# One tile for the output's sums, weight sums and additions at other slots, a branch's number loaded sooner, and two changes of order

## The chip, the cores and the metric

The kernel runs on one core of a Trainium2 chip. The metric is the device time of one execution in microseconds. Five engines work side by side and wait for each other by semaphores: TensorE (PE, with its weight loads PEld), VectorE (DVE), ScalarE (ACT), GpSimd (POOL) and SyncE (SP, which here only issues DMAs).

## The reference

A block of two layers on x of 8 x 256 tokens, 512 wide, all in float32:

```
xn = layernorm(x)
x  = x + attention0(xn) + ffn0(xn)      # layer 1
xn = layernorm(x)
x  = x + attention1(xn) + ffn1(xn)      # layer 2
```

`attention0` is a linear attention with 32 heads of 128 and decays: q, k, v = silu(xn @ W), scores weighted by a decay, the output normalized by its root mean square over all heads, multiplied by a weight and by sigmoid(xn @ Wg), and projected back to 512. `ffn0` routes each token to 2 of 16 experts, beside a shared expert. `attention1` is a softmax attention with one head of 128, `ffn1` a low-rank mixture: 16 of 64 rank-16 pairs for each token.

## The kernel before

**Opening.** The 2048 tokens are taken in four chunks of 512 (`NCH` = 4, `TPC` = 4 tiles of 128). Each chunk is normalized, turned with TensorE (`turn_rows`: four transposes into a PSUM bank, then a copy to SBUF, on VectorE for even tiles and on ScalarE, L282, for odd ones), routed, and sent through the shared expert (`shared_up`, `shared_down`). `decays` computes the decay tiles with ScalarE's Exp (L406) and stores them. Then VectorE works out which token goes to which slot of which expert. The opening's tiles lie in a pool, `opening`, that is closed behind that work; the attention's pool takes the same memory.

**Attention of layer 1.** Four passes, one for each chunk (`i`), of eight units, one for each group of four heads (`g`). A unit is seven `Outer` products (`ORDER`: p1, p2, p6, p5, p3, p7, p4; `k` counts them), and each of these again seven products of 8 matmuls of 128x128x128 (L738). This is a fast scheme of matrix multiplication with seven products in place of eight, used twice. The sums that it needs of weights and tokens are made in the first pass and stored in DRAM for the others. `copied` (L1112) takes a bank to SBUF with ScalarE; `result` adds banks and copies into the tiles a, b, c, d of the unit, on VectorE and GpSimd (all through `add`, L101). For p7, r is added to c on GpSimd and to a on VectorE; the additions to a are held in `self.added` and all made at the third quarter of the result, (1, 1), the last at (0, 1).

When a tile is whole, a `Quarter` begins: silu and gate on ScalarE (L835 to L842), `scores` (L860, L861, weighted into `s` on VectorE), `attend` (L872, L873), the squares `sq` (ScalarE, L884) that GpSimd adds into `sums`, and the gated output `gT`. `project` (L950) multiplies `gT` with the output weights `wo`, again in seven products p1 to p7, and adds each to its slice of the tile `acc`; in a pass's first unit it copies instead, on ScalarE (L958). At a pass's end `combine` (GpSimd) makes the four output blocks of the seven sums, in place, and `finish` (VectorE, L649) scales them and adds them to the tokens' sum. `acc` is made anew for each pass, in a pool with one buffer.

In the second pass (`i` = 1) `out_sum` makes the four weight sums p7, p5, p6 and p4 of each unit's `wo` on GpSimd and stores them in `wos`, from which later passes load.

**The order.** Within the attention ScalarE and GpSimd follow the program's order; TensorE, VectorE and SyncE are ordered by the framework's scheduler, which takes what is ready, in the program's order where several are. `keep_in_program_order` pins an instruction behind what was traced before it on its engine. Small steps are queued by hand: `later(n, f)` puts f into a list, and `slot()`, called after each product, runs what is due; there are 49 slots in a unit. Per slot one step runs, or two if more than 12 are waiting; names in a list (`out_sum`, `combine` and others) do not count.

**Experts.** From the second pass on, experts' tiles are gathered and computed between the products. 36 tiles are usual; a branch (`beyond`, L1215 and L1216) runs more if the data need them. Its number, `used`, is loaded into the engines' registers just ahead of the branch, in unit 3 of the last pass.

**Layer 2.** For each chunk: `low_rank` twice (L1614), then seven products (L1711) by `seven`, which runs lists of other work (`fill`) between its products: transposes of the next chunk (`turned`, L279), its routing (L1503), projections (L1492) and softmax.

## Time and profile before

| | |
|---|---|
| median of 3 runs | 2756.16 us (2751.43 to 2757.16) |
| profiled execution | 2759.92 us, span 2758.2 us |
| PE busy | 2704.0 us (98%) |
| VectorE, GpSimd, ScalarE busy | 1597.3, 1652.5, 943.9 us |
| matmuls | 19250 |
| granted clock of TensorE | 0.994 |

The profile is of one execution, which took longer than each of the three runs that were timed. Busy times are unions of the instructions' spans; an engine's idle time is told with what ended it. A line such as L101 is that of a helper (`tt`), so groups are told apart by their tiles, whose buffer numbers are left out. The opening lasts to about 120 us, the attention's four passes to about 2460 us, layer 2 to the end.

### The profile page before, as it was taken

Reading aid. Unit: us, or ns where it says so; the run is one execution under the profiler, and the core shown is the slowest. Engines: PE = TensorE matmul, PEld = TensorE weight load, DVE = VectorE, ACT = ScalarE, POOL = GpSimd, SP = SyncE. Lnnn points to the kernel's source line nnn. Section 1 sums busy time; section 2 is a strip of 40 time slices with the busy share of each in tenths; the row PEclk is TensorE's granted clock in tenths of the full one; section 3 lists DMA queues with packets and bytes.
Section 4 is the critical chain, followed back from the end, with each engine's and each line's share of the span. In section 5 each row is a group of like instructions: output and inputs, shape, how many; then the busy total and the mean of one; then the engine's idle time right before and its main releaser. Section 6 shows DMA issues by size and latency. Waiting matters only on the chain. (4 is left out here: it accounts for less than half of the span.)

```text
span 2758.2 us, 48688 instructions
## 1 busy us (share of the span) xinstructions
PE 2704.0 (98%) x19250; PEld 2499.6 (91%) x19250; DVE 1597.3 (58%) x2701; ACT 943.9 (34%) x1672; POOL 1652.5 (60%) x1509
## 2 busy tenths in 40 slices
PE   9999999999999999999999999999999999999999
PEld 5699999999999999999999999999998999987877
DVE  7656777776545555555545555555454555667663
ACT  5232222222343333333433333334433333432211
POOL 6478777776466767666755555656655567653210
PEclk9999999999999999999999999999999999999999
DMA  7898888888888777667777776787776688653211
GB/s 290 314 345 323 317 330 330 326 319 323 340 286 293 265 277 275 256 243 285 279 255 260 252 260 251 265 297 254 267 266 231 241 301 300 220 222 104 75 60 64
DMA packets 150872, 721.46 MB, mean 262 GB/s; under 512 B 18240, under 2 KB 24768, under 8 KB 108096
## 3 DMA queue, kind: packets, MB, share of 16 engines
q1 hardware_dynamic: 135824, 661.89, 65.2%
q0 software_dynamic: 14528, 55.88, 6.1%
q8 instruction: 154, 2.52, 0.4%
q14 instruction: 78, 0.64, 0.1%
q10 hardware_dynamic: 288, 0.52, 0.1%
HBM read 576.29 MB, written 144.04 MB: 261 GB/s over the span
## 5 line engine op out<-in xcount | busy, mean ns | idle before, releaser
L738 PE MATMUL ps_a<-xt,w 128*128 128x128 f32 x5376 | 752.1, 277 | 16.6 <-ACT cp L1112 11.8
L738 PEld LDWEIGHTS ps_a<-xt,w 128*128 128x128 f32 x5376 | 687.3, 193 | 44.5 <-ACT cp L1112 16.0
L101 POOL TENSOR_TENSOR c<-c,r 128x512 f32<-128x512 f32 x264 | 362.4, 1396 | 161.2 <-DVE r L101 157.7
L101 POOL TENSOR_TENSOR c<-c 128x512 f32<-128x512 f32 x240 | 305.8, 1286 | 254.4 <-DVE c L101 230.5
L1112 ACT COPY cp<-ps_a 128x512 f32<-128x512 f32 x384 | 224.2, 584 | 645.9 <-PE ps_a L738 620.0
L738 PE MATMUL ps_e<-xt,w 128*128 128x128 f32 x2688 | 376.1, 277 | 0.2 <-DVE r L101 0.2
L101 POOL TENSOR_TENSOR sums<-sums,sq 128x256 f32<-128x256 f32 x240 | 180.3, 751 | 307.7 <-ACT sq L884 297.9
L738 PE MATMUL ps_a<-w,xt 128*128 128x128 f32 x1792 | 348.0, 276 | 0.0
L738 PEld LDWEIGHTS ps_e<-xt,w 128*128 128x128 f32 x2688 | 342.9, 193 | 3.6 <-DVE r L101 0.4
L101 POOL TENSOR_TENSOR w<-w 128x512 f32<-128x512 f32 x224 | 298.2, 1339 | 76.4 <-DVE w L101 29.1
L950 PE MATMUL ps_sc<-wo,gT 128*128 128x256 f32 x1288 | 306.9, 382 | 5.2 <-PEq L1216 3.8
L738 PEld LDWEIGHTS ps_a<-w,xt 128*128 128x128 f32 x1792 | 273.3, 193 | 0.0
L101 DVE TENSOR_TENSOR acc<-ps_sc,acc 128x512 f32<-128x512 f32 x208 | 142.7, 689 | 207.0 <-PE ps_sc L950 164.2
L950 PEld LDWEIGHTS ps_sc<-wo,gT 128*128 128x128 f32 x1288 | 233.9, 192 | 31.6 <-issue 4.4
L893 DVE SCALAR_TENSOR_TENSOR gT<-ps_o,nw,c 128x256 f32<-128x256 f32 x256 | 112.0, 479 | 231.0 <-ACT sq L884 230.9
L738 PE MATMUL ps_b<-xt,w 128*128 128x128 f32 x1536 | 215.6, 277 | 6.0 <-issue 3.8
L101 DVE TENSOR_TENSOR c<-ps_a,c 128x512 f32<-128x512 f32 x216 | 146.8, 687 | 123.3 <-PE ps_a L738 117.6
L835 ACT ACTIVATE c<-c 128x512 f32<-128x512 f32 x256 | 150.2, 628 | 165.5 <-DVE c L101 108.0
L884 ACT ACTIVATE sq<-ps_o 128x512 f32<-128x512 f32 x128 | 76.5, 597 | 380.2 <-PE ps_o L873 371.8
L738 PEld LDWEIGHTS ps_b<-xt,w 128*128 128x128 f32 x1536 | 196.5, 193 | 9.2 <-issue 5.6
L101 DVE TENSOR_TENSOR s<-ps_sc,decay 128x384 f32<-128x384 f32 x256 | 139.1, 552 | 75.7 <-PE ps_sc L861 74.1
L738 PE MATMUL ps_e<-w,xt 128*128 128x128 f32 x896 | 174.1, 276 | 0.0
(296 smaller groups left out, 4581.7 us busy)
## 6 DMA issues: line engine op xcount, KB each, us to landing
w<-in_w_att_dram SPq DMA_DIRECT2D x56, 1024.0 KB
w<-in_w_att_dram SPq DMA_DIRECT2D x72, 768.0 KB
st<-in_w_att_dram SPq DMA_DIRECT2D x32, 1024.0 KB
wo<-in_w_out_dram SPq DMA_DIRECT2D x113, 256.0 KB
decay<-dec SPq DMA_DIRECT2D x64, 384.0 KB
w<-ws0p SPq DMA_DIRECT2D x12, 1792.0 KB
w<-ws1p SPq DMA_DIRECT2D x12, 1792.0 KB
w<-ws2p SPq DMA_DIRECT2D x12, 1792.0 KB
```

Source lines behind the costliest of these rows:

```text
L101: (eng or nc.vector).tensor_tensor(o, a, b, op)
L738: mm(bank[:, bass.ts(ty, P)], a, b, start=(first and ty == 0), stop=True, skip_group_check=True,)
L835: nc.scalar.activation(qk, qk, AF.Silu)
L884: nc.scalar.activation(sq, po, AF.Square)
L893: nc.vector.scalar_tensor_tensor(gT[:, h, :].rearrange("p (t n) -> p t n", t=2), po[:, bass.ts(h, S)].rearrange("p (t n) -> p t n", t=2), ...
L950: mm(py[:, bass.ts(t, S)], self.O[p][:, hh, bass.ts(t, P)], self.wo[p][:, hh, :], start=(t == 0 and hh == 0), stop=(hh == 1), skip_group_c ...
L1112: nc.scalar.copy(c, bank)
```

## The change

- `acc` becomes one tile for all passes, made once (`sums_of_seven`).
- The load of p3's output weights is asked for at `k` = 4 of a unit instead of 5; `out_sum`'s four steps are queued from there, 6, 22, 24 and 26 slots later, instead of 6, 8, 10 and 12 slots after `k` = 5.
- p7's additions to a: at (1, 1) the first is made at once and the next two one and two slots later (`add_a`, a name that does not count); the one of (0, 1) as before.
- The branch's number is loaded one unit earlier.
- In the opening, the first chunk's copies on ScalarE are pinned in program order, and the pool is closed before the slots are worked out.
- In layer 2, the first two of the next chunk's four transposed tiles move from ahead of `seven` into its first list, behind the first product.

```
-    def turn_rows(xT, xn, t, pt):
+    def turn_rows(xT, xn, t, pt, kept=lambda ins: ins):
...
-            nc.scalar.copy(o, i)
+            kept(nc.scalar.copy(o, i))
...
-            turn_rows(xT[i], xns[i], t, ps_mm())
+            turn_rows(xT[i], xns[i], t, ps_mm(), *(() if i else (tc.keep_in_program_order,)))
...
     share(NCH - 1, ups[-1])
+
+    opening.close()
...
-    opening.close()
-
...
+    whole_acc = []
+
+    def sums_of_seven():
+
+        if not whole_acc:
+            whole_acc.append(accp.tile([P, 7, 2, C // 2], FP, tag="acc", name="acc"))
+        return whole_acc[0]
...
                 if self.i not in acc:
-                    acc[self.i] = accp.tile([P, 7, 2, C // 2], FP, tag="acc", name="acc")
+                    acc[self.i] = sums_of_seven()
...
-                for p in {2: ("p1",), 3: ("p7", "p4", "p5"), 4: ("p6", "p2"), 5: ("p3",)}.get(k, ()):
+                for p in {2: ("p1",), 3: ("p7", "p4", "p5"), 4: ("p6", "p2", "p3")}.get(k, ()):
...
-                if k == 5 and self.i == 1:
+                if k == 4 and self.i == 1:
                     for n in range(4):
-                        later(6 + 2 * n, partial(self.out_sum, n))
+                        later((6, 22, 24, 26)[n], partial(self.out_sum, n))
...
+        def add_a(a, r):
+            add(a, a, r)
...
-                        self.added.append(partial(add, a, a, r))
-                        if (i, j) in ((1, 1), (0, 1)):
-                            while self.added:
-                                self.added.pop(0)()
+                        self.added.append(partial(add_a, a, r))
+                        if (i, j) == (1, 1):
+                            for n in range(3):
+                                later(n, self.added.pop(0)) if n else self.added.pop(0)()
+                        elif (i, j) == (0, 1):
+                            self.added.pop(0)()
...
-            n_used = nc.values_load(used[0:1, 0:1], min_val=0, max_val=NMT)
-            with tc.If(n_used > USUAL):
+            with tc.If(n_used[0] > USUAL):
...
+            if (i, g, k) == (NCH - 1, NG - 6, 1):
+                n_used.append(nc.values_load(used[0:1, 0:1], min_val=0, max_val=NMT))
             if (i, g, k) == (NCH - 1, NG - 5, 1):
...
-            turned(0)
-            turned(1)
             head = Head(i + 1)
-            fill = {1: [partial(turned, 2), partial(turned, 3)], 2: [fourth, head.route], 7: [head.qk], 3: [head.softmax], 4: [head.gates]}
+            fill = {1: [partial(turned, t) for t in range(TPC)], 2: [fourth, head.route], 7: [head.qk], 3: [head.softmax], 4: [head.gates]}
```

More of the change, by code (lines that the diff above doesn't have):

```diff
@@ L764, in slot @@
                 f()
-                n += getattr(f, "func", f).__name__ not in ("bias_sum", "silu", "bias", "gate", "fill_tile", "read_table", "take_table", "scatter", "load_sum", "sums1", "sums2", "sums3", "sums4", "settle0", "settle1", "out_sum", "combine", "finish", "store")
+                n += getattr(f, "func", f).__name__ not in ("add_a", "bias_sum", "silu", "bias", "gate", "fill_tile", "read_table", "take_table", "scatter", "load_sum", "sums1", "sums2", "sums3", "sums4", "settle0", "settle1", "out_sum", "combine", "finish", "store")
         class Expert:
@@ L974, in project_plain @@
                 if self.i not in acc:
-                    acc[self.i] = accp.tile([P, 7, 2, C // 2], FP, tag="acc", name="acc")
+                    acc[self.i] = sums_of_seven()
                 o = acc[self.i][:, 2 * b : 2 * b + 2, t]
@@ L1211, in fill_tile @@
             nc.sync.dma_start(out=yd[bass.ts(j, P), :], in_=x[0:P, :])
+        n_used = []
         def beyond():
-            n_used = nc.values_load(used[0:1, 0:1], min_val=0, max_val=NMT)
-            with tc.If(n_used > USUAL):
+            with tc.If(n_used[0] > USUAL):
                 for j in range(USUAL, NMT):
```

## The prediction

> **What bounds the kernel now.** I read the page first, then TensorE's list of waits, then the timeline around each long entry of that list. The page's first line says that TensorE sets the time:

> ```profile
> PE 2704.0 (98%) x19250; PEld 2499.6 (91%) x19250; DVE 1597.3 (58%) x2701; ACT 943.9 (34%) x1672; POOL 1652.5 (60%) x1509
> ```

> The span is 2758.2 us, so PE is idle for 54.2 us. The change takes no matmul away and adds none: it can win only idle time of PE, and what a slow clock behind such idle time costs. TensorE's waits (engine, line, what ended the wait: total us, times, longest) name its own candidates:

> ```profile
> PE ps_a L738 <- ACT cp L1112: 11.8, 6, 2.6
> PE ps_o L872 <- DVE s L101: 6.2, 6, 2.6
> PE ps_sc L279 <- DVE spare L259: 4.3, 5, 1.2
> PE ps_sc L950 <- PEq L1216: 3.8, 1, 3.8
> PE ps_b L360 <- ACT xT L282: 2.6, 1, 2.6
> ```

> The first row is the largest: PE waits for ScalarE's copies out of PSUM (`copied`). ScalarE is never short of time (34%), so something holds its queue. Five of the six waits lie in the attention passes: at 1156.19, 1230.73, 1305.27, 1360.30 and 1938.35 us (1.77, 1.77, 1.11, 2.65, 2.65 of idle). The timeline at 1360, all engines but the weight loads:

> ```profile
> 1352.33 2.17 DVE L649 SCALAR_TENSOR_TENSOR spare<-acc,rms,spare 128x512 f32<-128x512 f32 x2
> 1353.91 1.72 POOL L101 TENSOR_TENSOR acc<-acc 128x512 f32<-128x512 f32 x1
> 1355.66 3.41 DVE L649 SCALAR_TENSOR_TENSOR spare<-acc,rms,spare 128x512 f32<-128x512 f32 x2 [0.56 <-POOL acc L101]
> 1359.18 0.58 ACT L958 COPY acc<-ps_sc 128x512 f32<-128x512 f32 x1 [8.66 <-DVE spare L649]
> 1360.30 0.38 PE L738 MATMUL ps_a<-xt,w 128*128 128x128 f32 x1 [2.65 <-ACT cp L1112]
> ```

> The first write of the next pass's `acc` (L958) stands 8.66 us at the head of ScalarE's queue until the last `finish` (L649) of the pass before has read the old tile; the copies behind it, and then PE, stand too. 1938 is the same place one pass later, also 8.66. At 1156 it is another chain, told from GpSimd's timeline:

> ```profile
> 1143.80 1.26 POOL L101 TENSOR_TENSOR wo<-wo 128x512 f32<-128x512 f32 x1
> 1145.03 3.40 POOL L101 TENSOR_TENSOR c<-c,r 128x512 f32<-128x512 f32 x2
> 1148.39 3.07 POOL L101 TENSOR_TENSOR wo<-wo 128x512 f32<-128x512 f32 x2
> 1151.42 1.27 POOL L101 TENSOR_TENSOR c<-c,r 128x512 f32<-128x512 f32 x1
> ```

> and from ScalarE's:

> ```profile
> 1152.72 1.15 ACT L835 ACTIVATE c<-c 128x512 f32<-128x512 f32 x2 [5.01 <-POOL c L101]
> ```

> Three of `out_sum`'s subtractions (wo<-wo) stand among p7's additions to `c`; the last of those ends at 1152.69, the Silu of `c` waits 5.01 us for it, and the copies queued behind the Silu reach PE at 1156.19. At 1230 and 1305 the rows repeat (5.00 each).

> **The half clock.** The granted clock stands in the seventh column of these windows (us; then busy time and count of PE, PEld, DVE, ACT, POOL; clock; DMA):

> ```profile
> 1938.35:1941.75 3.40, 3.40 (x17) 3.40 (x18) 0.00 (x0) 1.96 (x3) 0.00 (x0) 0.55 0.98 290
> 1156.20:1159.60 3.40, 3.40 (x26) 3.30 (x27) 1.99 (x4) 3.14 (x7) 2.96 (x4) 1.00 0.94 375
> ```

> Behind the stall at 1938 (2.65 idle) the clock is 0.55 for 3.4 us: (1 - 0.55) x 3.4 = 1.5 us more. Behind 1360 (the same 2.65) and 1156 it stays 1.00. So such a stall costs its idle time and sometimes 1.5. [...] The row decides: 2.65 us were enough once in two.

> **One tile for the output's sums.** The copy L958 then waits only for readers of its own slice: p1's, index 4. `finish` reads indices 0 to 3; `combine` reads 4 in its first two steps, the second of which GpSimd ends at 1340.1. That overlap is judged by slice is in the rows above: the `finish` at 1352.33 started before the last `combine` (1353.91) of the same tile. PE's product for that copy ends at 1353.3, so the copy would run there, before the next `copied` is due. What was late behind it: VectorE, busy with `finish` until 1359.07, frees its bank of ps_a at 1359.67, while PE, not stopped, needs it three products later, near 1360.4. Both stalls go: 2 x 2.65 = 5.3, and 1.5 of clock: **6.8 us**. Bounds: 0 (slices not told apart in another place) to 8.3 (the clock's 1.5 at both).

> **The second pass's weight sums.** A unit is 74.55 us (1143.80, 1218.35: the same step of two units) and 49 slots, 1.52 us each. The first sum moves 7 slots, 10.6 us, ahead, where GpSimd has idled 4.22 us before 1142.05; the load of its operand p3 is issued at 1107.99, far ahead, so p3's load at k=4 instead of 5 is free, as SyncE already issues it as soon as the tile is released. The other three move 7 slots back, to slots 50, 52 and 54, about 1157, 1160 and 1164. Without them the four additions to `c` follow each other: the last starts near 1147.5, 3.9 us sooner, and the Silu's 5 us wait shrinks to about 1. PE's 1.77, 1.77 and 1.11 go: **4.65 us**. Queued behind the moved sums are p4's and the first quarter's next steps on GpSimd (sums at 1160.08, gT at 1161.59, idle 2.34 before 1165.21): that idle time and the 5.5 us taken out ahead of it are the cover. The stores to `wos` on SyncE wait for GpSimd as before, 10.6 us later, ahead of weight loads that no PE wait names. Bounds: -4.65 to +10 (see the slower rival).

> **p7's additions at other slots.** The same instructions on VectorE, whose order the scheduler makes by readiness with program order as the rank. At 766.85 PE waits 2.56 for `s`, behind two such additions at 762.76 that took 3.47 while GpSimd worked. Now they rank one and two slots later, but the scores still rank behind them. I count **0**; bounds 0 to 3.7 (2.56, and 1.1 for the clock of 0.67 in the 3.4 us after it).

> **The branch's number sooner.** PE's sequencer at the branch (name, count: min/median/max ns):

> ```profile
> L1215 PEldq TENSOR_LOAD <-used x1: 490/490/490, 2103.3 to 2103.3; - x1
> L1216 PEldq COMPARE_BRANCH  x1: 5007/5007/5007, 2103.9 to 2103.9; - x1
> ```

> The stall of 3.76 is the branch's 5.0 less what PE had queued. Only the load before it moves: **0.6 us**, from 2103.3 to 2103.9. At the new place, a unit earlier, it takes each sequencer the same 0.5; PE's runs ahead of its work (1.2 us at the branch: 5.0 less 3.76), which hides it. [...] Bounds -0.5 to 0.6.

> **Opening and second layer.** PE's 2.59 at 13.28 waits for two copies (L282, 12.18) behind four decay activations (L406, 10.51 to 12.27). Pinning the copies behind what was traced before them forbids nothing to the decays, which are traced later: **0**; if they do come first, PE starts at about 11.4 instead of 13.28, 1.9, and (1 - 0.59) x 4.2 = 1.7 of clock: up to 3.6. Closing the pool sooner: SyncE's first load into it (L1017) leaves at 124.34, when the store xr<-x has landed; that store stays: 0. In the second layer TensorE's timeline shows that the transposes already come after the first product:

> ```profile
> 2512.65 0.59 PE L1711 MATMUL ps_a<-fb,hg 128*128 128x256 f32 x2
> 2513.08 0.59 PE L1711 MATMUL ps_b<-fb,hg 128*128 128x256 f32 x2
> 2513.51 1.04 PE L279 MATMUL ps_sc<-ident,spare 128*128 128x128 f32 x8
> 2515.71 0.96 PE L279 MATMUL ps_sc<-ident,spare 128*128 128x128 f32 x6 [0.73 <-DVE spare L259]
> ```

> ps_a is p1, ps_b p2. Program order catches up with issue order: **0**, bounds 0 to the five waits' 4.3.

> **Sum.** 6.8 + 4.65 + 0.6 = 12.05. The profiled execution took 2759.92, so its like would take 2747.9. It is 3.76 above the median 2756.16, about two and a half windows at half clock; from the median I forecast 2756.16 - 12.05 = **2744.1 us**.

> **Rivals.** *More goes* (0.17): the opening's 3.6, the 3.7 at 766 or the layer's 4.3; for it, the waits are there and the scheduler ranks everything anew; against, the order of issue that I read says nothing moves. All three give 2732.5, the middle about 2737. *One source only* (0.13): a new wait takes the place of one. For it: the chains are long and VectorE's and TensorE's orders are made anew. The tile alone gives 2756.2 - 7.4 = 2748.8, the sums alone 2756.2 - 5.25 = 2750.9. *It does nothing* (0.08): slices of one tile are not told apart and the sums only shift the wait: 2755. *Slower* (0.06): the three sums of 1.27 us now stand on GpSimd before the gT that p7's product needs. gT ends at 1162.86, the product starts at 1164.28: past 1.42 us of lateness PE waits. If each of eight units then pays 1.77, and half of them 1.5 of clock, that is 14.2 + 6 = 20.2 against 7.4 won: 2769. Against it: four sums are ahead of that gT now, at most two afterwards.

> **How the numbers follow.** The central case has 0.56. About what a measurement here can tell from no change is 0.2%, 5.5 us: faster means under 2750.6. Central, more, and half of the one-source case: 0.56 + 0.17 + 0.07 = 0.80; the other half and nothing: 0.14; slower 0.06. The range goes from all extras (2732.5, and 1.5 for one more window of full clock) to the sums alone with some loss: 2731 to 2753.

> **What would show it.** Right: L958 no longer waits for L649, and no PE wait at the two pass changes; no Silu wait of 5 us in the second pass's last three units; the branch still at 5.0; 13.28 and 766.85 still there. Wrong: PE waits on `cp`, `gT` or `s` at new places in the second pass, or the half clock in more windows.

## The result, and the profile after

The changed kernel takes 2740.93 us (median of 6 runs, 2735.27 to 2743.35); the kernel before took 2753.84 us beside it (6 runs). The ratio is 0.9946, with a 95% interval of 0.9936 to 0.9957: 14.9 us less (11.8 to 17.6). (The ratio is taken over the runs and isn't the quotient of the medians, which lie 12.9 us apart.) The forecast was 12.05 less and 2744.1 us.

The profiled execution of the changed kernel is the fastest of its runs (2735.27 us), that of before was slower than all that were timed (2759.92 us). So the two traces differ by 24.7 us, about twice what the medians do (12.9): part of what they show is chance, and has to be told apart. The line numbers of the changed kernel that are named here are the old ones (L101, L279, L282, L360) or higher by 7 to 15: the products L738 are L745, `copied` L1112 is L1122, the first write of `acc` L958 is L965, `finish` L649 is L656, the Silu L835 is L842, the branch L1216 is L1229.

The page's first line (busy us, share, instructions), and rows of TensorE's list of waits (total us, times, longest):

```profile
PE 2695.3 (99%) x19250; PEld 2492.6 (91%) x19250; DVE 1590.8 (58%) x2701; ACT 944.9 (35%) x1672; POOL 1652.1 (60%) x1509
```
```profile
PE ps_sc L957 <- PEq L1229: 3.4, 1, 3.4
...
PE ps_a L745 <- ACT cp L1122: 2.7, 3, 1.8
PE ps_b L360 <- ACT xT L282: 2.6, 1, 2.6
```

PE is idle for 38.3 us of its span instead of 54.2. The row that led the list, 11.8 us for ScalarE's copies, is down to 2.7: 1.8 of it lies near 125 us, in the opening, the rest is 0.46 and 0.45 at the two pass changes. The branch (PEq) and the opening's wait for `xT` are where they were. The pass change, on ScalarE and on VectorE:

```profile
1341.18 0.59 ACT L965 COPY acc<-ps_sc 128x512 f32<-128x512 f32 x1 [2.98 <-PE ps_sc L957]
```
```profile
1343.34 3.42 DVE L656 SCALAR_TENSOR_TENSOR spare<-acc,rms,spare 128x512 f32<-128x512 f32 x2 [0.56 <-POOL acc L101]
```

The copy into `acc` no longer stands 8.66 us behind `finish`. It waits for PE's product alone, and is done at 1341.77, 1.6 us before the last two steps of `finish` start. In the second pass, GpSimd (`...` for the rows between) and ScalarE:

```profile
1135.17 6.94 POOL L101 TENSOR_TENSOR c<-c,r 128x512 f32<-128x512 f32 x4 [3.97 <-DVE r L101]
...
1146.36 1.29 POOL L101 TENSOR_TENSOR wo<-wo 128x512 f32<-128x512 f32 x1
```
```profile
1142.14 1.15 ACT L842 ACTIVATE c<-c 128x512 f32<-128x512 f32 x2 [1.30 <-POOL c L101]
```

The four additions to `c` follow each other without a sum among them, and take 6.94 us from the first to the last where they took 10.64 (1142.05 to 1152.69); the first sum has gone into GpSimd's idle time ahead (1127.48), the second follows them, the last two stand behind the next `gT` (1152.87). The Silu waits 1.30 us instead of 5.01, and PE's waits of 1.77, 1.77 and 1.11 are gone.

What these two places are worth can be had more exactly than from the whole time. PE runs 19250 products in every trace, and between its 5600th and its 14400th product, from the second pass to the fourth, its times in the traces agree to 0.03 us wherever no wait and no half clock differ. What differs from execution to execution lies ahead of that stretch and behind it. Its time in us for the same products, with the runs of the next section beside (a star: the granted clock is at half behind the pass change):

| products | before | changed | tile alone | sums alone | rest alone |
|---|---|---|---|---|---|
| 5600 to 9600, second pass | 528.58 | 521.87 | 530.37 | 521.87 | 528.71 |
| 9600 to 10400, pass change | 105.34 | 102.95 | 102.93 | 106.58* | 106.60* |
| 10400 to 13600 | 418.37 | 418.37 | 418.37 | 418.38 | 418.37 |
| 13600 to 14400, pass change | 108.03* | 104.39 | 104.38 | 106.78 | 108.01* |

The sums take 6.7 us off the second pass. The tile takes 2.4 us off each pass change, and with it the 1.25 us that a half clock costs there where one follows (106.58 against 105.34, 108.03 against 106.78). The 530.37 of the tile alone holds a half clock behind its wait near 1227 us, which the kernel before had not.

What did not move is to be seen as well. PE's sequencer at the branch:

```profile
L1388 PEldq TENSOR_LOAD <-used x1: 492/492/492, 2085.0 to 2085.0; - x1
L1229 PEldq COMPARE_BRANCH  x1: 4627/4627/4627, 2085.6 to 2085.6; - x1
```

The number's load is traced a unit sooner, and on GpSimd and ScalarE, which follow the program, it did move (to 2012.0 and 2012.5, some 70 us ahead of the branch). On TensorE, which the scheduler orders, it is still issued 0.6 us ahead of it. And VectorE at p7's additions in the first unit of the second pass:

```profile
758.77 3.47 DVE L101 TENSOR_TENSOR c<-c,r 128x512 f32<-128x512 f32 x2
762.17 1.01 DVE L101 TENSOR_TENSOR s<-ps_sc,decay 128x384 f32<-128x384 f32 x2
```

They still stand ahead of `s`, at the same 3.47 us. PE waits 1.91 there instead of 2.56, and a new 0.42 for `r` 4 us ahead; both are in the run of the sums alone too, and neither in that of the rest alone (2.56), so they come of the sums. The opening's 2.59 is there too, and TensorE's order in layer 2 is the one of before.

### The profile page after: what moved, and what is told of

Read it like the earlier page. It is cut to its first block, busy times and chain, and to the rows that moved or that the text cites. A ratio compares the mean times of both kernels' runs of the same rounds, so it can differ in the third digit from the quotient of the medians.

```text
span 2733.6 us, 48695 instructions
## 1 busy us (share of the span) xinstructions
PE 2695.3 (99%) x19250; PEld 2492.6 (91%) x19250; DVE 1590.8 (58%) x2701; ACT 944.9 (35%) x1672; POOL 1652.1 (60%) x1509
## 5 line engine op out<-in xcount | busy, mean ns | idle before, releaser
L745 PE MATMUL ps_a<-xt,w 128*128 128x128 f32 x5376 | 749.4, 276 | 6.9 <-POOL w L101 3.2
L745 PEld LDWEIGHTS ps_a<-xt,w 128*128 128x128 f32 x5376 | 685.7, 192 | 32.0 <-issue 14.6
L101 POOL TENSOR_TENSOR c<-c,r 128x512 f32<-128x512 f32 x264 | 362.1, 1397 | 158.5 <-DVE r L101 151.4
L1122 ACT COPY cp<-ps_a 128x512 f32<-128x512 f32 x384 | 224.6, 585 | 673.6 <-PE ps_a L745 633.5
L101 POOL TENSOR_TENSOR c<-c 128x512 f32<-128x512 f32 x240 | 305.9, 1287 | 248.6 <-DVE c L101 221.5
L745 PE MATMUL ps_e<-xt,w 128*128 128x128 f32 x2688 | 374.5, 275 | 0.2 <-DVE r L101 0.2
L101 POOL TENSOR_TENSOR sums<-sums,sq 128x256 f32<-128x256 f32 x240 | 181.0, 754 | 295.6 <-ACT sq L891 285.8
L745 PE MATMUL ps_a<-w,xt 128*128 128x128 f32 x1792 | 346.6, 275 | 0.0
L745 PEld LDWEIGHTS ps_e<-xt,w 128*128 128x128 f32 x2688 | 341.5, 192 | 4.5 <-issue 1.0
L101 POOL TENSOR_TENSOR w<-w 128x512 f32<-128x512 f32 x224 | 298.4, 1340 | 74.3 <-DVE w L101 28.1
L745 PEld LDWEIGHTS ps_a<-w,xt 128*128 128x128 f32 x1792 | 272.3, 192 | 0.0
L101 DVE TENSOR_TENSOR acc<-ps_sc,acc 128x512 f32<-128x512 f32 x208 | 142.6, 689 | 211.2 <-PE ps_sc L957 167.5
L745 PE MATMUL ps_b<-xt,w 128*128 128x128 f32 x1536 | 214.9, 276 | 5.6 <-issue 3.5
L101 DVE TENSOR_TENSOR c<-ps_a,c 128x512 f32<-128x512 f32 x216 | 146.6, 686 | 114.6 <-PE ps_a L745 108.5
L745 PEld LDWEIGHTS ps_b<-xt,w 128*128 128x128 f32 x1536 | 195.6, 193 | 8.6 <-issue 5.2
L842 ACT ACTIVATE c<-c 128x512 f32<-128x512 f32 x256 | 150.1, 627 | 140.1 <-DVE c L101 106.3
L101 DVE TENSOR_TENSOR s<-ps_sc,decay 128x384 f32<-128x384 f32 x256 | 139.4, 552 | 79.6 <-PE ps_sc L868 78.2
L745 PE MATMUL ps_e<-w,xt 128*128 128x128 f32 x896 | 173.5, 275 | 0.0
```

What stands on the lines that cost most here:

```text
L101: (eng or nc.vector).tensor_tensor(o, a, b, op)
L745: mm(bank[:, bass.ts(ty, P)], a, b, start=(first and ty == 0), stop=True, skip_group_check=True,)
L842: nc.scalar.activation(qk, qk, AF.Silu)
L1122: nc.scalar.copy(c, bank)
```

## The experiments

Each is compared with the kernel before in runs on the same chip. Its medians there are 2757.08 us beside the first four runs, 2755.38 beside the three on the sums and the last one (decays and additions together), 2756.92 beside the other four. Differences in us are the ratio's difference from 1 by that median. The changed kernel itself did not run beside them: a comparison with it sets ratio against ratio.

### Its parts: the tile, the sums, the rest

**One tile alone.** `acc[self.i] = sums_of_seven()`, all else as before.

> The kernel before with one tile for the output's sums, and nothing else of the change. Theory (two separate causes): PE's two waits of 2.65 at the pass changes, near 1360 and 1938 us, go; the three near 1156, 1230 and 1305 (1.77, 1.77, 1.11) stay, and so does Silu's wait of 5.0 on ScalarE. 6.8 us less than the kernel before, about 2747 beside its 2754. Rival (the gain lies in the order made anew, at the end of the first pass near 650 us and in fewer half-clock windows): the two waits go, but less than 4 us are won. Rival (one chain): a wait that goes comes back elsewhere in the pass, within 0.2% of before.

Ratio 0.9968 (0.9956 to 0.9981): 8.8 us less (5.2 to 12.1).

```profile
PE ps_a L745 <- ACT cp L1119: 7.6, 6, 1.9
```

The two waits at the pass changes fell from 2.65 to 0.45 each; the other three are there with 1.77, 1.88 and 1.12. The theory holds; the one-chain rival does not, nor does the rival of less than 4 us.

**The sums alone.**

```
-                for p in {2: ("p1",), 3: ("p7", "p4", "p5"), 4: ("p6", "p2"), 5: ("p3",)}.get(k, ()):
+                for p in {2: ("p1",), 3: ("p7", "p4", "p5"), 4: ("p6", "p2", "p3")}.get(k, ()):
...
-                if k == 5 and self.i == 1:
+                if k == 4 and self.i == 1:
                     for n in range(4):
-                        later(6 + 2 * n, partial(self.out_sum, n))
+                        later((6, 22, 24, 26)[n], partial(self.out_sum, n))
```

> The kernel before with the second pass's weights' sums at their new slots and p3's load with k=4, nothing else. Theory (two separate causes): ScalarE's Silu waits about 1.3 us instead of 5.0 at three units, PE's waits near 1156, 1230 and 1305 go, the two of 2.65 at the pass changes stay, with L958 still waiting 8.66 for the finish. 4.65 us less than before, about 2749 beside 2754. Rival (order made anew): under 3 us. Rival (slower): sums ahead of gT on GpSimd make PE wait for p7's product, up to 15 us more.

Ratio 0.9958 (0.9944 to 0.9973): 11.6 us less (7.4 to 15.4).

```profile
PE ps_a L738 <- ACT cp L1112: 7.1, 3, 2.6
```

The converse: the three waits are gone, the two of 2.65 (and the opening's 1.84) are there. But the time is less by more than the 4.65 that was expected, which lies outside the interval, and by more than the 6.7 of the table above. The next group comes back to that.

**The rest alone**: p7's additions, the branch's number, the opening's and the second layer's order, without the tile and the sums.

> The change without its two large parts: a tile of sums for each pass and the weights' sums at the old slots, as before; p7's additions, the branch's number, the opening's and the second layer's order as in the change. Theory: nothing that can be told, at most 0.6 us; all five waits of the second pass are there, and PE's idle time stays within 1 us of the 54.2 before. Rival (order made anew): the end of the first pass near 650 us, where PE waited 1.68 and 2.02 before and 1.78 once after, loses its second wait here too, and about 4 to 5 us are won.

Ratio 1.0 (0.999 to 1.0011). Nothing, as the theory had it. All five waits are there. The rival does not hold: near 650 us PE waits twice here too, 0.67 and 2.02 us where it was 1.68 and 2.02 before and 1.78 alone after. The shorter first wait is not a matter of order either: VectorE runs the same steps in the same order there in these traces, and waits ahead of them for a load of weights (`st`): 2.32 us in the kernel before, 1.32 in this one, not at all in the changed kernel, 2.16 in a later variant of the changed kernel. How late that load lands differs from trace to trace, and not with the edits.

**Tile and sums together.**

> The kernel before with the one tile and the sums' new slots together, nothing of the rest. Theory: all of the change's gain, 11.5 to 13 us less than before, within 0.1% of the changed kernel; the five waits are gone. Rival (order made anew): 4 to 5 us of the gain are missing, and the two waits near 650 us (1.68 and 2.02) are as in the kernel before. Rival (one chain): no more than either part alone.

Ratio 0.9938 (0.9923 to 0.9953): 17.1 us less (13.0 to 21.2), not to be told from the whole change's 0.9946, and the stretch of the table is the changed kernel's to 0.01 us in each row. The two parts are the change. Near 758 us VectorE's timeline of this kernel is the changed kernel's, 2.35 us later and else alike to 0.02 us, although p7's additions are queued as before: their new slots do nothing there.

### Which of the sums

**Only the first of the four ahead**, on the kernel before: `later((6, 15, 17, 19)[n], ...)` from `k == 4`, so that the last three keep their places.

> The kernel before with only the first of the four sums moved ahead (and p3's load with it); the other three stay at their old slots among p7's additions. Theory (the Silu waits for p7's additions as long as sums stand among them): the chain is shorter by one sum of 1.27, the Silu waits about 3.7 instead of 5.0, PE's waits shrink from 1.77, 1.77, 1.11 to about 0.5, 0.5, 0: 3.6 of the 4.65 are won. Rival (all the gain is in the three that move behind): the waits stay within 0.3 of what they were. On the clock, for this run and the three beside it: the half-clock windows lie on one grid of 3.41 us, each follows a cell of it in which PE idled more than 1.9 us, and no cell with less than 1.75 is followed by one; the rival is the length of the single wait, whatever its place on the grid.

Ratio 0.9979 (0.9968 to 0.9991): 5.8 us less (2.5 to 8.8).

```profile
1140.84 1.71 POOL L101 TENSOR_TENSOR wo<-wo 128x512 f32<-128x512 f32 x1
1142.52 1.71 POOL L101 TENSOR_TENSOR c<-c,r 128x512 f32<-128x512 f32 x1
```
```profile
1144.27 1.15 ACT L835 ACTIVATE c<-c 128x512 f32<-128x512 f32 x2 [2.43 <-POOL c L101]
```

One sum is still among the four additions, not three: with the first gone, the additions are ahead of the others. The Silu waits 2.43, not the expected 3.7, and that is short enough for all three of PE's waits to be gone. In the four units ahead of these it waits 4.29, more than the 2.58 of the kernel before, and PE loses nothing there: how much of the Silu's wait reaches PE differs from unit to unit.

**Only the last three behind**: `later((6, 15, 17, 19)[n], ...)` from `k == 5`.

> The kernel before with only the last three of the four sums moved behind p7's additions; the first stays. Theory: the first still delays the additions by 1.27, but the last of them ends about 3 us sooner, so the Silu waits about 2.5 and PE not at all: the 4.65 are won whole, near 2747 to 2752 beside 2757. Rival (the second pass's sums give 11 us by themselves, as the run with all four moved showed, by something that is not these three waits): 9 to 12 us less than before although the trace shows no more than the three waits gone.

Ratio 0.9978 (0.9966 to 0.999): 6.1 us less (2.8 to 9.4). The Silu waits 2.42; PE's three waits are gone. So either half of the edit takes all of PE's waits away; the other half only makes the Silu's slack larger. This run leaves the load of p3's weights where it was, so that load has no part in it.

Both halves together gave 11.6 alone (7.4 to 15.4), where these give 6; the intervals overlap. The traces give all three the same: the 4000 products of the second pass take 521.87 us with all four sums moved, 522.36 with the first alone, 521.88 with the last three. That is 6.7 less than before, 2.05 more than the three waits: 0.8 lies in what follows them, and 1.2 in the units near 855, 930 and 1010 us, in each of which PE got through its products 0.4 us sooner, though its list for the kernel before names no wait there above 0.05. What else differs in the trace with all four sums, against the run of the rest alone on the same chip, lies elsewhere: a half-clock window near 1936 us fewer but one near 765 more, and in layer 2 no wait of 1.94 with a half clock behind it, where VectorE waits 1.53 for a late load of `spread_g`. Such things differ from trace to trace here. The rival (11 us by something that is not these waits) did not show in either half; why six runs of the whole lay so low stays open.

**Three sums together ahead of `gT`**, on the changed kernel: slots (6, 20, 20, 20).

> The changed kernel with the last three sums together ahead of p7's last two additions and of the gT that p7's product needs, so three sums stand ahead of that gT on GpSimd instead of one. Theory (the slack there is 1.77 us: gT ends at 1152.93 and its product starts at 1154.70): two more sums are 2.6 us, so gT comes 0.8 late or more in the units where GpSimd has no idle time before it; PE waits for gT or for the copy behind a late Silu, 2 to 8 us more than the changed kernel. Rival (GpSimd's idle time takes them up): no new wait over 0.5, within 1 us of the changed kernel.

Ratio 0.9983 (0.9974 to 0.9993), some 10 us slower than the changed kernel's 0.9946; the intervals are apart.

```profile
PE ps_sc L957 <- POOL gT L101: 8.0, 5, 2.2
```
```profile
784.15 2.72 PE L957 MATMUL ps_sc<-wo,gT 128*128 128x256 f32 x8 [2.22 <-POOL gT L101]
```

Four of the eight units now wait for `gT` (2.22, 1.80, 1.79 and 0.84 us; the fifth wait, 1.4, is in a later pass and stood in the kernel before too), and at 784 a half-clock window stands behind it. This is the prediction's slower rival brought about: the mechanism is real, and the price, some 10, is above the 2 to 8 expected, if not by more than the noise. In the changed kernel only one sum is ahead of that `gT`, and 1.77 us of slack are left.

### What the change did not move

**The decays pinned**, on the changed kernel, so that the copies of `xT` go first:

```
+                if n < 3:
+                    tc.keep_in_program_order(ins)      # ins: the Exp of the decays, L406
```

> The changed kernel with the first three pairs of decay activations pinned behind what is traced before them, so that ScalarE makes the two copies of xT first. Theory (the pin of the copies alone moved nothing; the decays ahead of them cost PE its wait at 13.28 us): PE starts 1.7 to 1.9 us sooner and a half-clock window may go: 2 to 3.6 us less than the changed kernel, about 2738 beside its 2741. Rival (the opening's end waits for the loads or for the store of xr, not for PE): the wait of 2.59 goes, the one near 125 us grows by as much, and the time stays within 1 us.

Ratio 0.994 (0.9927 to 0.9953), the same as the changed kernel's.

```profile
11.36 3.70 PE L360 MATMUL ps_b<-xT,wsh 128*128 128x512 f32 x8 [0.67 <-ACT xT L282]
```

PE starts at 11.36 instead of 13.71, at full clock. Then the rival takes over: a new wait of 0.9 for VectorE at 30 us, and the wait near 125 us grows from 1.84 to 2.5. Of the 2.35 us won at the start 1.1 are left behind the wait near 125 (124.38 instead of 125.51), too little to be told.

**p7's additions four slots later and pinned**, on the changed kernel.

> The changed kernel with p7's additions four slots later than the change puts them and pinned to program order, so that on VectorE the scores' steps (s) come before the last of them. Theory (the change's own slots leave VectorE's order as it was, so the additions won nothing; moved in earnest they would): s no longer waits behind two additions of 1.7 us near 758 to 762, PE's wait of 1.9 there falls under 0.5, and 1.5 to 3 us less than the changed kernel. Rival (the additions are wanted soon after): what reads their sums is late instead, on PE or ScalarE, and nothing or up to 5 us more.

Ratio 0.9935 (0.9922 to 0.9948): at best 3 us below the changed kernel, not told apart.

```profile
758.49 1.57 DVE L1081 TENSOR_TENSOR c<-c,r 128x512 f32<-128x512 f32 x1
760.48 1.21 DVE L101 TENSOR_TENSOR s<-ps_sc,decay 128x384 f32<-128x384 f32 x2 [0.41 <-PE ps_sc L868]
```

Moved in earnest, the scores come first and PE's 1.91 at 763 is gone, but other waits grow or come, both for `r`: 0.78 at 758 (0.42 in the changed kernel) and 1.1 at 2421. What was won at one reader is lost at the next.

**The second layer's transposes behind p2**, the routing behind p6.

> The changed kernel with the second layer's transposes put behind p2's product and the routing behind p6's. Theory (the change's own new order was already PE's order, so it won nothing; PE's waits of 0.57 to 0.92 for the normalised rows are real): these waits, 0.59, 0.57, 0.92 and 0.84 in three chunks, go, and 2 to 2.9 us less than the changed kernel. Rival (the chain over the routing to the next chunk's attention sets the pace): PE waits later in the chunk, at the products of q and k or at the gates, and the time is the same or up to 3 us more.

Ratio 0.9963 (0.9949 to 0.9977), some 5 us slower than the changed kernel's ratio, though the intervals overlap.

```profile
PE ps_sc L1519 <- DVE yT L284: 2.7, 1, 2.7
PE ps_sc L1519 <- DVE wsm L284: 2.7, 1, 2.7
```

PE's four small waits for the normalised rows went, and two of 2.7 came in the projections that read the turned rows. The waits are the rival's: it is the chain to the next chunk's attention that sets the pace there.

**No branch.** The branch and its load are left out.

> The changed kernel without the branch and without the load of its number; what it would do with more than the usual expert tiles is left out. Theory (the branch itself, not the load, is the stall): PE's wait of 3.4 near 2090 us goes, 3.4 to 5 us less than the changed kernel, the larger if the half-clock window behind it was in its timed runs too. Rival (PE runs into the next wait there, for GpSimd's gT): under 2 us less.

Ratio 0.9921 (0.9905 to 0.9938), 6.9 us below the changed kernel's ratio; the intervals just overlap. PE's wait there is gone from the trace. The branch itself is the stall, not the load of its number, which lasts 0.49 us. In the thirteen traces that have it, PE's compare-and-branch lasts 3.96 to 5.29 us.

**Decays and additions together**, both as above.

> The changed kernel with both later changes that did no harm: the decays pinned behind the copies of xT, and p7's additions behind the scores and pinned. Theory: the wait for s near 763 us stays gone, PE starts 2 us sooner in the opening and gives most of it back near 30 and 124 us: 2736 to 2740, 1 to 5 us less than the changed kernel. Rival (what is won early is given back at the next load that arrives late): same as the changed kernel within 1 us.

2738.12 us, ratio 0.994 (0.9925 to 0.9955): not told from the changed kernel either. None of the runs beats it by more than the intervals allow; the one that leaves the branch out comes nearest.

## Why the prediction was right, and where it was not

*One tile, 6.8 us.* Right in mechanism: slices of one tile are told apart by the scheduler's waits, so the copy waits only for its own slice. Measured alone: 8.8 (5.2 to 12.1). Two details of the term were off and nearly cancel. The waits did not go to 0 but to 0.45 each, because the copies are still queued behind other work of ScalarE (in the changed kernel the steps on `c`, 1348.74 to 1351.68, ahead of PE's wait that ends at 1352.21); PE's products there took 2.4 us less each time, not 2.65. And the half clock behind such a wait is not one of two at these two places, but a matter of place on a grid (below): six of the ten waits of 2.65 in the five traces that have them are followed by it, and it cost 1.25 there, not 1.5. That makes 2 x 2.4 + 2 x 0.6 x 1.25 = 6.3.

*The sums, 4.65 us.* Right in mechanism, too small in size: Silu's 5.0 became 1.30 (about 1 was said), the three waits went, and in that pass nothing but 0.42 for `r` came in their place. But the second pass is shorter by 6.7 (528.58 to 521.87): the waits alone were counted, not the 0.8 us in what follows them nor the 1.2 us in earlier units. The halves measured 5.8 and 6.1; the whole alone 11.6, of which some 5 stay open. The additions end 3.7 us sooner after their start (6.94 against 10.64), 3.9 were said. What was not seen is that either half of the edit would have done.

*The branch's number, 0.6 us.* Wrong. I took the number's load to move with its place in the program. On TensorE the scheduler orders it, and left it right ahead of the branch (2085.0 and 2085.6). The stall did fall, by 0.37, but only because that execution's branch took 4.63 instead of 5.01 us; the kernels without this edit show 2.8 to 3.9 for the same wait.

*p7's additions, opening, second layer: 0 each.* Right, all three: the order is unchanged, what little the waits differ is not their doing, and the rest alone measured 1.0 (0.999 to 1.0011). The bounds above them, 3.7, 3.6 and 4.3, were not to be had even when the order was moved in earnest.

*The sum.* The two terms as the traces give them make 6.3 + 6.7 = 13.0, inside the measured 14.9 (11.8 to 17.6); the 1.9 between can't be told from noise. The forecast of 12.05 has 0.5 too much for the tile, 2.05 too little for the sums and 0.6 for the branch that did not come: that it is as near as this is in part luck. In the profiled pair the difference beyond that is chance: 1.9 of idle near 650 us (the load of `st`), three half-clock windows that come and go between traces, 1.4 for rows in layer 2. The forecast was taken from the median, not from the slow profiled execution, and that was right: from the latter it would have been 2747.9.

*"What would show it"* came out as said, but for 0.45 us left at each pass change, the branch at 4.6 instead of 5.0, and 1.91 in place of 2.56 for the wait at 766.85.

## What to carry to other kernels

A queue that has the time may still be late (ScalarE was busy for 34% and stood 8.66 us at each of two pass changes): look for the one instruction at its head, and ask whether it waits for data or only for a buffer. The buffer made anew for each pass waited here for all readers of the old one, and PE 2.65 us behind it; one tile for all passes waited slice by slice, and PE 0.45. Before counting on an edit of program order, see whether the engine follows the program or a scheduler; where it was a scheduler, the edits here that changed no readiness changed nothing (the rest alone, ratio 1.0), and one that did moved the wait to the next reader (1.91 for `s` went, 0.78 and 1.1 for `r` stood there).

## What the runs showed of the hardware

```profile
1355.03:1358.44 3.41, 2.62 (x24) 2.43 (x22) 2.85 (x3) 0.00 (x0) 3.41 (x3) 1.00 0.35 107
1358.44:1361.85 3.41, 1.55 (x13) 1.55 (x14) 1.23 (x2) 1.86 (x4) 1.76 (x2) 1.00 0.62 231
...
1935.30:1938.71 3.41, 0.76 (x7) 0.57 (x6) 2.42 (x3) 1.48 (x3) 2.94 (x2) 1.00 0.27 111
1938.71:1942.12 3.41, 3.41 (x19) 3.41 (x18) 0.18 (x1) 1.96 (x4) 0.00 (x0) 0.50 0.96 283
```

The wait of 2.65 at 1360 is cut by the grid into 0.79 and 1.86, and the clock stays; the one at 1938 lies in one cell (0.76 busy, 2.65 idle), and the next cell is at half clock. In the changed kernel even the branch's 3.39 is cut into halves (1.63 and 1.75) and costs no clock:

```profile
2085.34:2088.76 3.42, 1.79 (x17) 1.60 (x15) 1.38 (x2) 0.99 (x2) 0.00 (x0) 1.00 0.64 265
2088.76:2092.17 3.41, 1.66 (x8) 1.51 (x9) 0.00 (x0) 0.59 (x1) 0.00 (x0) 1.00 0.23 52
2092.17:2095.58 3.41, 3.41 (x28) 3.28 (x27) 0.69 (x1) 0.59 (x1) 0.00 (x0) 1.00 0.83 267
```

So in these traces a wait's clock cost is not a fixed price but a chance that goes by the idle time in one cell: of the full-clock cells with more than 1.94 of 3.41 us idle every one is followed by a half clock, with 1.75 to 1.94 about half, with 0.5 to 1.75 none.

**This compare-and-branch took PE's sequencer 3.96 to 5.29 us** over the thirteen traces, where the other engines' took 45 to 72 ns (before and after). Why PE's is so long no run here shows. Without the branch the ratio was lower by 6.9 us, with intervals that just overlap. A half clock followed the branch in the trace of before (0.52 in 2109.25 to 2112.65) and not in that of the changed kernel (1.00 in 2092.17 to 2095.58).
